# A gated two-layer transformer block in fp32: the second pass's query projection by two levels of seven products

## The chip, the cores and the metric

The kernel runs on one core of a Trainium2 chip. The metric is the device time of one execution in microseconds; the median over several runs counts, and lower is better. All arithmetic is fp32.

## The reference

The input `x` is 8 batches of 256 tokens with 1024 features. Four residual layers follow each other, each gated by a tanh: an autocorrelation attention against a context, a feed-forward layer with low-rank additions, a cross-attention, and a last feed-forward layer. The change concerns the third:

```python
q = (layernorm(x) @ wq).reshape(bs, s, 32, 128).transpose(0, 2, 1, 3)   # 32 query heads
k = (ctx @ wk).reshape(bs, s, 8, 128).transpose(0, 2, 1, 3)             # 8 key heads
v = (ctx @ wv).reshape(bs, s, 8, 128).transpose(0, 2, 1, 3)
q, k = rope(q), rope(k)
w = softmax(where(mask, q @ k.T / sqrt(128), -1e9))     # four query heads per key head
x = x + tanh(g) * ((w @ v) @ wo)
```

`wq` is 1024 x 4096 and `wo` is 4096 x 1024.

## The kernel before

**Passes and steps.** The 8 batches are done in two passes of four batches (1024 tokens), and each pass goes through all four layers. In the cross-attention a pass has two blocks of 512 tokens (two batches each) and 8 key heads. A step is one block and one key head: it makes the queries of the four query heads (`queries`, L968), the scores and softmax (`scores`, L1124), the weighted values (`values`, L1161), and then the output projection (`outputs` L989 in the first pass, `outputs_of_two` L1016 in the second). The 16 steps go block by block, and in each block head by head.

**Seven products.** The large projections use a scheme that multiplies two matrices cut into 2 x 2 quarters by seven products of quarters instead of eight. It needs sums of quarters on both sides beforehand (`left_operands` L206 for weights, `right_operands` L215 for tokens: four sums each) and sums of the products afterwards (`combine`, L223: per seven products one copy on ScalarE and seven sums on VectorE). The order of the products is `SEVEN = (1, 2, 6, 7, 4, 5, 3)`. For the queries the quarters are over 512 of 1024 features and two of four heads, and over tokens of one batch of the block's two. A product then is two accumulation groups of four matmuls of 128 x 128 by 128 x 256, into a PSUM tile of the pool `at_mm`, which has four (L855). The output projection of the second pass uses two levels of this scheme, 49 products for a pair of key heads, with weight sums (`wo2_d`) that the first pass makes on GpSimd (`finer_weights`, L912) and keeps in HBM.

**Rope.** `combine` leaves each finished quarter of the queries in PSUM. `rope` (L709) then takes three operations on VectorE that read it (L714 to L716) and one addition on GpSimd (L717), and the tile with the queries is ready for the scores.

**Sums of tokens and weights.** `query_operands` (L824) normalizes a block (VectorE), transposes it (TensorE, copies on ScalarE) and makes the token sums (VectorE). The first pass's steps over its first block make the sums of `wq` and `wo` (VectorE, L863 and L885) and store them in HBM (`wq_d`, `wo_d`); later steps load them.

**Order.** The code is written as generators. In each step the four quarter-steps `(n, l)` do scores, then a number of products of the next step's queries (`q_fill`), then values of the quarter-step before with some products of the outputs (`o_fill`) in between. A scheduler then places the instructions on each engine, so that an engine's queue differs somewhat from the order in the code. Each engine works through its queue in order, and all transfers shown here are issued from SyncE's (SP) queue, in order too; an SP transfer that waits holds up those behind it.

Of the kernel before, what the change touches and what calls it, by code (L numbers as in the profile page):

```python
# [46 lines left out]
def flamingo_kernel(ctx: ExitStack, tc: tile.TileContext, a: dict, out: bass.AP):  # L47
# [54 lines left out]
    wo2_d = [dram.tile([P, 7, 2, 2, 2, S], F32, name=f"wo2_d{i}") for i in range(N_KV // 2)]  # L102

# [249 lines left out]

    def normed(dst, xt, mv, rstd, i):
        nc.vector.tensor_scalar(
            dst, xt, mv[:, i, 0:1], rstd[:, i : i + 1], ALU.subtract, ALU.mult
        )
# [25 lines left out]
    def autocorrelation(p, xt, pools, beside, late):  # L383
# [12 lines left out]
        def normalize(b0, b1):  # L396

            n = b1 - b0
            mv, rstd = norm_stats(xt[b0 * 2 : b1 * 2])
            lin = stats.tile([P, 2 * n, 2], F32, tag="lin", name="lin", bufs=2)  # L400
            nc.vector.tensor_copy(lin[:, :, 0], rstd[:, : 2 * n])
            nc.vector.scalar_tensor_tensor(
                lin[:, :, 1], mv[:, : 2 * n, 0], -1.0, rstd[:, : 2 * n], ALU.mult, ALU.mult
            )
            for b in range(n):
                norms[b0 + b] = lin[:, b * 2, :], lin[:, b * 2 + 1, :]
# [302 lines left out]
    def rope(dst, x, cos, sin, pool):  # L709

        H = P // 2
        t = pool.tile([P, 2, S], F32, tag="rope", name="rope", bufs=1)
# [136 lines left out]

    def attention(p, xt, groups, keep, norms, xops, ahead):  # L850
        gq, go, gx = groups
        with (
# [8 lines left out]
            paired = p == NPASS - 1  # L861

            def load_wq(step):  # L863
# [12 lines left out]
                else:  # L876
                    ops = {}
                    where = {1: a["wq"][g, 0, 0], 2: a["wq"][g, 0, 1], 4: a["wq"][g, 1, 1]}
                    where |= dict(zip((5, 7, 6, 3), wq_d[g]))
                    for r in SEVEN:  # L880
                        ops[r] = big_tile(gq, [2, KH, DH], f"wq_{r}")
                        nc.sync.dma_start(ops[r], where[r])
                wq[step] = ops

# [45 lines left out]
            def stream_wo():  # L930

                places = []
                for _, g in steps[::2]:
                    for n, r in enumerate(SEVEN):
# [33 lines left out]
            def queries(step, qT):  # L968
# [3 lines left out]
                for r in SEVEN:  # L972
# [11 lines left out]
                    if done:  # L984
                        qT[done[1]] = half("qT", 7)
                        rope(qT[done[1]], done[0], tab_q[:, 0, :], tab_q[:, 1, :], w1)
                    yield

# [204 lines left out]
            fine = nothing  # L1193
            new_xl = lambda: big_tile(gx, [D], "xl")
            if paired:
                wo_stream = stream_wo()
            load_wq(steps[0])
            load_kv(steps[0])
            qT = {}
            for _ in queries(steps[0], qT):  # L1200
                pass
            norms[1] = norm_stats(xt[NBT:])
            load_wq(steps[1])
# [3 lines left out]
            if paired:  # L1207
                q_fill = {0: (2, 2, 1, 1), 1: (2, 2, 2, 1), end: (0, 0, 0, 0)}
                o_fill = {k: (0, 5, 10, 10) if k % 2 == 0 else (3, 5, 8, 8) for k in range(end)}
                o_fill[end] = (6, 6, 6, 6)  # L1210
# [6 lines left out]
            def start_outputs():  # L1217
                if paired:
                    got = outputs_of_two(last[0][0][0], [oT for _, oT in last])
# [7 lines left out]
            for k, step in enumerate(steps):  # L1227
                follow = k + 1 < len(steps)
                following = {}
                if follow:  # L1230
                    load_kv(steps[k + 1])
                    q_gen = queries(steps[k + 1], following)
                    if k == 0:
                        fill_from(q_gen, 1)
                else:
                    q_gen = nothing
                for i, (n, l) in enumerate(((0, 0), (0, 1), (1, 0), (1, 1))):
                    got = scores(step, l, n, qT)
                    nq = q_fill.get(k, (3, 3, 1, 0))[i]
                    no = o_fill[k][i]  # L1240
                    fill_from(q_gen, nq)
                    mid = min(no, middle)
                    if i > 0:
                        fill_from(o_gen, no - mid)
                    if before is not None:
                        values(*before, lambda: fill_from(o_gen, mid))
# [7 lines left out]
                    if i == 2 and k + 2 < len(steps):  # L1254
# [7 lines left out]
                    if i == 0 and p == 0 and step[0] > 0 and step[1] % 2:  # L1262
                        fine = finer_weights(step)
# [313 lines left out]
```

## Time and profile before

| what | value |
|---|---|
| median of 3 runs | 3332.11 us (3331.08 to 3334.94) |
| the profiled execution | 3335.22 us, its span 3333.4 us |
| TensorE busy | 3265.3 us, 98% |
| VectorE busy | 2217.8 us, 67% |
| GpSimd busy | 1412.0 us, 42% |
| ScalarE busy | 1051.6 us, 32% |
| moved by DMA | 505.55 MB, mean 152 GB/s |
| cross-attention, first pass | its first queries start at 534.7 us |
| cross-attention, second pass | its first queries start at 2205.9 us, its last output products at about 3227 us |

A matmul in fp32 shows up as two instructions in the trace. TensorE's matmuls overlap, so that the mean time of one (379 ns for 128 x 256) is longer than the distance between two of them. A stretch's row names, in this order, its length, the busy time and number of instructions of TensorE, of its weight loads, of VectorE, ScalarE and GpSimd, the granted TensorE clock, the share of the DMA engines and GB/s. A row of groups has the line, engine, operation, tiles and shapes, the count, the busy time and the mean of one in ns, and then the engine's idle time before these instructions with what ended it.

### The profile page before, as it was taken

The page shows a single profiled execution, that of the slowest core. Times are in us where ns is not written, and L with a number is a line of the kernel's source. Part 1 is how long each engine was busy: PE and PEld are TensorE (multiplying, and loading weights), DVE is VectorE, ACT ScalarE, POOL GpSimd, SP SyncE. Part 2 cuts the span into 40 slices and gives each one's busy share as a digit, 9 for nine tenths or more (in the row PEclk, how much of TensorE's full clock was granted, in tenths as well). Part 3 has the DMA queues.
Part 4 walks back from the last instruction along what each step waited for, and adds up shares of the span by engine and source line. Part 5 has one row for each costly group of instructions (what it writes and reads, how often), then busy time and mean ns, then how long its engine had stood idle before and what let it go on. Part 6 is the DMA issues. An engine that isn't in the chain of part 4 may idle for free. (4 is left out here: it accounts for less than half of the span.)

```text
span 3333.4 us, 39399 instructions
## 1 busy us (share of the span) xinstructions
PE 3265.3 (98%) x13456; PEld 2406.4 (72%) x13456; DVE 2217.8 (67%) x4305; ACT 1051.6 (32%) x2555; POOL 1412.0 (42%) x1181
## 2 busy tenths in 40 slices
PE   8999999999999999999999999999999999999999
PEld 6677557777677767775456677568888888888874
DVE  7787757867776655564647686456676766666773
ACT  1333112433333433334113231115333334334420
POOL 4554211333322475476344542112454454454662
PEclk9999999999999999999999999999999999999999
DMA  7533705333333354554443434043554455555551
GB/s 278 175 117 120 273 32 193 136 130 137 135 125 128 133 212 152 175 206 161 144 162 117 144 115 165 7 163 99 164 184 160 161 169 173 167 168 171 177 187 51
DMA packets 216933, 505.55 MB, mean 152 GB/s; under 512 B 25204, under 2 KB 103028, under 8 KB 216734
## 3 DMA queue, kind: packets, MB, share of 16 engines
q1 hardware_dynamic: 215582, 498.84, 44.2%
q0 software_dynamic: 1152, 4.19, 0.3%
q8 instruction: 108, 1.77, 0.2%
q14 instruction: 91, 0.75, 0.1%
HBM read 394.96 MB, written 108.00 MB: 151 GB/s over the span
## 5 line engine op out<-in xcount | busy, mean ns | idle before, releaser
L717 POOL TENSOR_TENSOR qT<-qT,rope 128x512 f32<-128x512 f32 x128 | 170.0, 1328 | 786.9 <-DVE qT L716 747.1
L976 PE MATMUL ps_q<-xn,wq 128*128 128x256 f32 x1920 | 428.9, 379 | 0.0
L976 PEld LDWEIGHTS ps_q<-xn,wq 128*128 128x128 f32 x1920 | 364.8, 190 | 50.5 <-PE po L677 0.5
L1146 ACT ACTIVATE s<-s,nmx 128x256 f32<-128x256 f32 x512 | 255.9, 500 | 244.7 <-DVE nmx L1143 244.5
L1141 DVE COPY_PREDICATED s<-keep,ps_s 128x512 f32<-128x512 uint8 x256 | 184.9, 726 | 156.4 <-PE ps_s L1132 155.5
L976 PE MATMUL ps_q<-xn_t,wq 128*128 128x256 f32 x1280 | 285.6, 379 | 0.0
L370 DVE SCALAR_TENSOR_TENSOR x<-po,tg,x 128x512 f32<-128x512 f32 x248 | 177.3, 743 | 136.8 <-PE po L677 42.2
L976 PEld LDWEIGHTS ps_q<-xn_t,wq 128*128 128x128 f32 x1280 | 243.2, 190 | 33.1
L1173 ACT COPY wT<-pt 128x512 f32<-128x512 f32 x256 | 138.8, 585 | 362.4 <-PE pt L1167 362.4
L1132 PE MATMUL ps_s<-kT,qT 128*128 128x256 f32 x1024 | 247.9, 379 | 0.0
L1178 PE MATMUL av<-wT,v 128*128 128x256 f32 x1024 | 245.7, 382 | 1.7 <-ACT wT L1173 1.6
L1155 ACT ACTIVATE s<-s,tot 128x256 f32<-128x256 f32 x512 | 230.2, 497 | 39.9 <-DVE tot L1153 39.8
L1178 PEld LDWEIGHTS av<-wT,v 128*128 128x128 f32 x1024 | 191.4, 190 | 54.6 <-issue 22.2
L1068 PE MATMUL po<-wo,oI 128*128 128x256 f32 x896 | 215.6, 381 | 2.0 <-issue 1.2
L1132 PEld LDWEIGHTS ps_s<-kT,qT 128*128 128x128 f32 x1024 | 191.8, 190 | 25.1 <-issue 0.5
L1005 PE MATMUL po<-wo,oT 128*128 128x512 f32 x448 | 201.3, 592 | 0.0
L1068 PEld LDWEIGHTS po<-wo,oI 128*128 128x128 f32 x896 | 169.2, 191 | 25.7 <-issue 2.0
L1186 ACT COPY oT<-av 128x512 f32<-128x512 f32 x128 | 74.9, 585 | 355.1 <-PE av L1178 353.5
L253 POOL TENSOR_TENSOR x<-x,part 128x512 f32<-128x512 f32 x48 | 75.3, 1570 | 249.1 <-ACT part L252 249.1
L1143 DVE TENSOR_REDUCE nmx<-s 128x2 f32<-128x512 f32 x256 | 173.2, 682 | 6.9
L1068 PE MATMUL po<-wo,oT 128*128 128x256 f32 x672 | 172.8, 384 | 1.9 <-DVE co L1083 0.3
L1005 PEld LDWEIGHTS po<-wo,oT 128*128 128x128 f32 x448 | 82.7, 190 | 82.5 <-issue 74.1
(290 smaller groups left out, 6401.7 us busy)
## 6 DMA issues: line engine op xcount, KB each, us to landing
wo<-wo_d SPq DMA_DIRECT2D x144, 512.0 KB, 4.6
wq<-in_wq_dram SPq DMA_DIRECT2D x104, 512.0 KB, 3.5
wq<-wq_d SPq DMA_DIRECT2D x96, 512.0 KB, 3.3
wo<-in_wo_dram SPq DMA_DIRECT2D x56, 512.0 KB, 3.5
wo_d<-fine_t SPq DMA_DIRECT2D x56, 512.0 KB, 3.3
wo<-wo_d SPq DMA_DIRECT2D x96, 256.0 KB, 3.5
w<-w_d SPq DMA_DIRECT2D x36, 512.0 KB, 5.7
wo<-in_wo_dram SPq DMA_DIRECT2D x72, 256.0 KB, 3.4
```

The source lines that it names most:

```text
L370: nc.vector.scalar_tensor_tensor(xs, ps, g, xs, ALU.mult, ALU.add)
L717: nc.gpsimd.tensor_add(dst, dst, t)
L976: nc.tensor.matmul(ps[:, l, :], wops[r][:, l, c, :], xo[r][:, c, :], start=(c == 0), stop=(c == KH - 1),)
L1005: nc.tensor.matmul(po, ops[r][:, h, t * P : (t + 1) * P], wops[r][:, h, :], start=(h == 0), stop=(h == 1),)
L1068: nc.tensor.matmul(po, left[r2][:, h, :], w[:, h, :], start=(h == 0), stop=(h == 1))
L1132: nc.tensor.matmul(ps[:, t, :], qT[i, n][:, l, t * P : (t + 1) * P], kT[:, n * S : (n + 1) * S], start=True, stop=True,)
L1141: nc.vector.copy_predicated(s, keep[b], ps)
L1143: nc.vector.tensor_reduce(nmx, s, AX.X, ALU.max, negate=True)
L1146: nc.scalar.activation(s[:, t, :], s[:, t, :], AF.Exp, bias=nmx[:, t : t + 1], accum_out=tot[:, t : t + 1],)
L1155: nc.scalar.activation(s[:, t, :], s[:, t, :], AF.Copy, scale=tot[:, t : t + 1])
L1173: nc.scalar.copy(wT[i], pt)
L1178: nc.tensor.matmul(av[:, i, :], kv[step][1][:, n * 2 + c, :], wT[i][:, c, :], start=(c == 0), stop=(c == 1),)
```

## The change

In the second pass the queries are made by two levels of seven products, for a pair of key heads and both blocks of tokens at once: the outer level cuts features, heads and tokens once (as before, but over both blocks and both key heads), the inner level cuts each of the seven products again. A pair takes 49 products of two groups of two matmuls; four pairs make 196 products, where 16 steps made 112 products of two groups of four. The steps of the second pass change their order to go through a pair of heads before the next.

- `finer_queries`: the first pass's steps over its first block load the weight operands of both heads of a pair, make four differences or sums for each of the seven (GpSimd), and store them in HBM (`wq2_d`). The stores of one round are issued at the start of the next.
- `second_block`: before the second pass's steps, the second block is normalized (ScalarE), transposed and summed (VectorE) while the first 14 products run, and both blocks' operands are combined: two differences each on VectorE and two on GpSimd, seven times, all stored in HBM (`x2_d`).
- `queries_of_all`: all 196 products, each with its weight operand and (after the first 14) its token operand loaded into one tile of a pool of seven; `combine` for the inner level, then sums of the outer level in PSUM or in kept tiles, and `rope`.
- `q_fill` and `o_fill` of the second pass are set anew, and one product of the queries is placed between the transposes and the values.

```diff
+            if paired:
+                order = (0, 0), (0, 1), (1, 1), (1, 0)
+                steps = [(blk, g + i) for g in range(0, N_KV, 2) for blk, i in order]
...
+            def finer_queries(g):
...
+                coming, before = load(0), None
+                yield
+                for n in range(7):
+                    q00, q01, q10, q11 = this = coming
+                    if before:
+                        store(n - 1, before)
+                    nc.gpsimd.tensor_add(q11, q10, q11)
+                    nc.gpsimd.tensor_sub(q10, q00, q10)
+                    if n < 6:
+                        coming = load(n + 1)
+                    yield
+                    nc.gpsimd.tensor_sub(q00, q11, q00)
+                    nc.gpsimd.tensor_sub(q01, q01, q00)
+                    before = this
+                    yield
+                store(6, before)
...
+            def second_block(kept, qT):
...
+                sums = Steps(nc.vector)
+                s = [big_tile(go, [KH, S], f"xn_t{i}") for i in (1, 2, 4)]
+                ops = right_operands(sums, q, *s)
+                late = {}
+                for n, r in enumerate(SEVEN):
+                    if n < 4:
+                        sums.run((0, 2, 1, 3)[n])
...
+                    nc.vector.tensor_sub(t1, b[1], b[0])
+                    nc.vector.tensor_sub(t2, b[3], t1)
+                    flat = [t.rearrange("p b s -> p (b s)") for t in (t1, t2)]
+                    nc.sync.dma_start(x2_d[n][3][:, 0], flat[1])
+                    nc.sync.dma_start(x2_d[n][2][:, 0], flat[0])
+                    late[n] = b, t2
+                    kept[0] += 1
+                    yield
+                while len(qT.get(steps[0], {})) < 4:
+                    yield
+                for n, r in enumerate(SEVEN):
+                    b, t2 = late[n]
+                    nc.gpsimd.tensor_sub(b[1], b[3], b[1])
+                    nc.sync.dma_start(x2_d[n][1], ops[r].rearrange("p (k c) s -> p k (c s)", k=2))
+                    nc.gpsimd.tensor_sub(t2, t2, b[2])
+                    nc.sync.dma_start(x2_d[n][4][:, 0], t2.rearrange("p b s -> p (b s)"))
...
+                    yield
+                kept[0] = 7 * 7 * N_KV // 2
...
+            def queries_of_all(kept, qT, places):
...
+                            while len(ops) < min(m + 7, kept[0]):
+                                load()
...
+                            for l in range(2):
+                                for c in range(KQ):
+                                    nc.tensor.matmul(
+                                        ps[:, l, :],
+                                        w[:, l, c, :],
+                                        x[:, c, :],
+                                        start=(c == 0),
+                                        stop=(c == KQ - 1),
+                                    )
+                            at = {2: (0, 0), 5: (1, 1), 3: (0, 1), 4: (1, 0)}.get(r)
+                            dest = lambda ps: u1[at] if r1 == 1 else ps
+                            done = combine(r, ps, tiles, lambda tag: half(tag, 1), dest)
+                            if done and r1 != 1:
+                                u, w = u1[at], w1_[at] if r1 in (7, 4, 5) else None
+                                if r1 == 7:
+                                    nc.vector.tensor_add(w, ps, u)
+                                if r1 in (6, 5):
+                                    nc.vector.tensor_add(u, ps, u)
+                                if r1 == 4:
+                                    nc.vector.tensor_sub(ps, w, ps)
+                                if r1 in (2, 5, 3):
+                                    nc.vector.tensor_add(ps, ps, w if r1 == 5 else u)
+                                if r1 in (2, 4, 5, 3):
+                                    step = {2: (0, g), 4: (0, g + 1), 5: (1, g + 1), 3: (1, g)}[r1]
+                                    q = next(places["q"])
+                                    rope(q, ps, tab_q[:, 0, :], tab_q[:, 1, :], w1)
+                                    qT.setdefault(step, {})[at] = q
+                            yield
...
+                q_gen = queries_of_all(kept, qT, places)
+                sums = second_block(kept, qT)
+                next(sums)
+                for _ in range(14):
+                    next(q_gen)
+                    next(sums)
+                for _ in sums:
+                    pass
...
-                q_fill = {0: (2, 2, 1, 1), 1: (2, 2, 2, 1), end: (0, 0, 0, 0)}
-                o_fill = {k: (0, 5, 10, 10) if k % 2 == 0 else (3, 5, 8, 8) for k in range(end)}
-                o_fill[end] = (6, 6, 6, 6)
+                q_fill = {k: (3 + (k % 4 == 1), 3, 3, 3) for k in range(end)}
+                q_fill[0] = 6, 6, 6, 6
+                q_fill |= {end - 2: (2, 2, 2, 1), end - 1: (1, 1, 1, 1), end: (0, 0, 0, 0)}
+                o_fill = {k: (4, 7, 7, 7) if k % 2 == 0 else (6, 6, 6, 6) for k in range(end + 1)}
...
+                    if i == 3 and p == 0 and k % 2 == 0 and k < N_KV:
+                        fine_q = finer_queries(k)
+                    fill_from(fine_q, 1)
```

In the first pass `queries` stays, and its `rope` gets two buffers instead of one.

## The prediction

> **What bounds the kernel now.** I read the engine totals first, then stretches of the second pass's attention (it runs from 2206 to about 3230 us), then who waits for whom in it, then the rows that price the edited operations. From the page:
>
> ```profile
> span 3333.4 us, 39399 instructions
> PE 3265.3 (98%) x13456; PEld 2406.4 (72%) x13456; DVE 2217.8 (67%) x4305; ACT 1051.6 (32%) x2555; POOL 1412.0 (42%) x1181
> ```
>
> TensorE (PE) is busy all the time: only less work there, or a new wait, moves the end. By stretch, the first being the first pass's steps over its first block, the others groups of steps of the second pass:
>
> ```profile
> 527.00:1000.00 473.00, 472.07 (x1950) 347.30 (x1949) 350.56 (x533) 169.50 (x447) 145.16 (x106) 1.00 0.40 142
> ...
> 2310.00:2543.00 233.00, 232.59 (x1128) 203.60 (x1127) 154.35 (x289) 89.03 (x240) 106.10 (x100) 1.00 0.50 161
> 2543.00:2778.00 235.00, 234.16 (x1152) 204.36 (x1151) 164.02 (x303) 91.24 (x242) 115.01 (x110) 1.00 0.53 171
> sum 968.00, PE 966.00 PEld 845.46 DVE 658.91 ACT 386.27 POOL 440.21; mean PE 161.00 PEld 140.91 DVE 109.82 ACT 64.38 POOL 73.37
> ```
>
> The columns are PE, weight loads, VectorE, ScalarE, GpSimd, clock, DMA share, GB/s. The reader is to see full TensorE, VectorE at 68% (658.9 of 968), and full clock. TensorE's waits in the whole stage are 3 us:
>
> ```profile
> PE po L1068 <- issue: 1.2, 1, 1.2
> PE po L1068 <- DVE co L1076: 0.8, 1, 0.8
> PE pt L365 <- DVE xn L355: 0.4, 1, 0.4
> ```
>
> The prices, from the groups by form and, last, TensorE's timeline:
>
> ```profile
> L244 DVE TENSOR_TENSOR ps_q<-ps_q,u 128x512 f32<-128x512 f32 x64 | 44.7, 698 | 109.0 <-PE ps_q L976 109.0
> L714 DVE TENSOR_TENSOR rope<-ps_q,tab_q 64x512 f32<-64x512 f32 x128 | 88.7, 693 | 6.8 <-POOL qT L717 0.7
> L717 POOL TENSOR_TENSOR qT<-qT,rope 128x512 f32<-128x512 f32 x128 | 170.0, 1328 | 786.9 <-DVE qT L716 747.1 <-DVE rstd L351 22.8 <-PE ps_s L1132 10.0
> L1095 DVE TENSOR_TENSOR co<-co 128x512 f32<-128x512 f32 x16 | 12.4, 774 | 0.0
> L211 DVE TENSOR_TENSOR wq_s<-wq_s,wq 128x1024 f32<-128x1024 f32 x8 | 16.9, 2114 | 0.0
> L209 DVE TENSOR_TENSOR wq_s<-wq,wq 128x1024 f32<-128x1024 f32 x8 | 9.7, 1219 | 1.4 <-DMA wq<-in_wq_dram 1.4
> ```
>
> ```profile
> 2219.68 7.07 PE L976 MATMUL ps_q<-xn_t,wq 128*128 128x256 f32 x32
> 2226.59 7.07 PE L976 MATMUL ps_q<-xn,wq 128*128 128x256 f32 x32
> ```
>
> Thirty-two matmul instructions start 6.91 us before the next 32: 0.216 us each. The 379 ns in a row are of overlapping ones.
>
> **The change, part by part.**
>
> TensorE. A step's queries were 7 products of 8 matmuls; 16 steps make 896. Now two key heads and both blocks take 49 products of 4, four times: 784. The 112 that go are 224 instructions of the trace: 224 x 0.216 = **-48.4 us**. The second block's 32 transposes (3.5 us), eight copies and four sums move from step 6 to the start, past the first scores; they are in the counts below. Groups of two matmuls instead of four should cost nothing: the outputs' groups are of two, and 8 of theirs take from 2645.88 to 2647.61, again 0.216.
>
> VectorE. For two heads and both blocks it combined 4 x 7 operations and turned 16 tiles of queries by 3: 76. Now the inner level takes 49, the outer 28, the ropes 48: 125. The 49 more, four times, are 196 x 0.69 = 135 us; 14 token differences at 0.77 add 11; four normalizations (0.96 each) go to ScalarE. Together +142: 801 us in about 920, or 87%. None of that is free unless TensorE never waits for it.
>
> Here a rule speaks against the change. Before, a step's queries kept PE 24.2 us and VectorE 19 x 0.69 = 13.1, and the trace shows TensorE waiting for VectorE for almost nothing; on that evidence the 48 us stay whole. The Trainium skill, "Trainium Kernel Development and Optimization", section Best Practices, warns that faster matmuls do not empty PSUM any faster. Now 49 products are 84.7 us of PE against 125 x 0.69 = 86.3 of VectorE: by the rule the queries run at VectorE's pace wherever no other matmuls stretch them. By the trace alone the next two items are 0 and the whole sum comes to -29; by the rule they cost 35. I go by the rule, since the row is of a ratio of 0.54 and this is 1.02. I counted the changed kernel's order of instructions by quarter-step (from one pair of score tiles to the next), each at its row's duration.
>
> - Steps 4 to 7: PE 238.4, VectorE 210.5 in all, but unevenly. The third and fourth quarter of step 4 and the first of step 5 hold PE 11.2 + 13.0 + 19.9 = 44.1 against VectorE 15.8 + 17.0 + 22.3 = 55.1. A product waits until the one four before it is emptied (`at_mm` has four tiles, and a tile is held through the outer sum and the three rope operations). Followed through these quarters, PE waits 3.2, 0.4 and 2.1 us, about 6; the last quarter of step 6 (11.2 against 15.8) adds 1. Steps 8 to 11 are the same. Steps 2 and 3 give 1, steps 12 to 15 about 4: **+19**.
> - The start: 14 products before the first scores, then steps 0 and 1. PE 124.4, VectorE 135.7, and VectorE comes 4.4 us late (it ends its old work at 2210.3, the queries start at 2205.9). Products 15, 16 and 17 wait for ropes, 3.5 + 3.7 + 1.8; later PE 24.2 meets VectorE 35.3, and with some 4 us of slack 7 go: **+16**.
> - There GpSimd's 14 differences run beside VectorE's 18 sums in SBUF. The row of L211 shows 2.11 us where its like takes 1.22: it runs while GpSimd adds (763.5 to 765.8, and GpSimd's two adds beside it take 2.51 and 2.25 instead of 1.27). If all 18 paid, 16 us (0.9 each); if none met, 0. Of the four sums that `left_operands` makes, L211 alone pays so, and the operations that read PSUM do not; about a third: **+5**.
> - The second level's rope has one buffer: the next waits for GpSimd's add, 1.33 us after. Two ropes often lie 1 to 1.5 us apart. Bounds: 0, and 64 x 0.7 (the only such wait in the trace) = 45 if all lay on the path. Only the dense quarters count: **+4**.
>
> The first pass. GpSimd gets 112 differences of 1.3 us, 146 us on top of 145 in 473; SyncE's queue gets 224 transfers of 256 KB, 58.7 MB: 142 GB/s becomes 266, the share 0.40 becomes 0.75. Behind a difference that waits for its load stand, on GpSimd, the rope's adds (for the scores), the outputs' operands and the residual adds; behind a store that waits for GpSimd stand, on SP, loads of `wq`, `wo`, keys and values. In a step from 732 to 798 us the `wo` loads land 28 us ahead of use and GpSimd has a hole of 24 us where 14 differences need 18; the closest rope add ends 6.5 us before its scores. Bounds: 0, and 5 us in each of 8 steps, 40. It is nearest to the holes: **+7**.
>
> Transfers of the second pass: a step's queries load 12.25 products x 2 x 0.262 = 6.4 MB instead of 7 x 0.524 = 3.7; with 6.4 of `wo` and 0.5 of keys and values it moves 13.3 MB instead of 10.6, 171 GB/s becomes 232, share 0.72. Twelve products in a row in step 0 want 6.3 MB in 20.7 us, 304 GB/s, where the busiest slice of the page moves 278: 2 us short, and the seven tiles ahead help: **+3** (0 to 15). Those loads read sums from HBM that must have landed; in SP's queue eleven stores that wait for GpSimd stand just ahead of them, and behind them keys, values and `wo`. The new order of the steps moves as many keys and values as before: 0.
>
> ScalarE (12 copies, 8 normalizations more) stays under half busy: 0; uncovered it would be 13 us.
>
> Sum: -48.4 + 19 + 16 + 5 + 4 + 7 + 3 = +5.6. The profiled execution took 3335.2 us (span 3333.4), 3.1 above the median of 3332.1. Against the median: **3338 us**.
>
> **The rivals.**
>
> *The tiles give slack enough.* VectorE's 87% stays under PE, TensorE waited 3 us in a stage where VectorE had single quarters at 80 to 100%, and GpSimd's holes take the differences. Then the stalls halve, 19 + 16 to 18, and the small terms come to 6: -48.4 + 24 = -24, 3308 us. Against it: three dense quarters in a row never occur before.
>
> *The first pass's queues block (slower).* A round of four differences reuses tiles whose stores must land (3.3 us) before the next loads (3.4) can start, then 5.2 us of work. Where a round holds GpSimd past the rope's margin of 6.5 us, TensorE waits for scores. At 2 us in half the quarter-steps of eight steps (16) that is 32 instead of 7: 3363 us. For it: one in-order queue, DMA at 0.75. Against: the 28 us margins of the weights.
>
> *It does not save what it says.* If short groups pay the 0.241 us that the busy time of L1068 gives (215.6 / 896) instead of 0.216, 1568 instructions lose 38 us: 3376. The timeline speaks against it.
>
> **How the numbers follow.** Forecast 0.51, its own range 3325 to 3352; slack 0.31; queues 0.15; no saving 0.03. A measurement here tells 0.2%, 6.7 us, from no change. The forecast gives 0.04 faster, 0.19 same, 0.28 slower; slack 0.30 faster, 0.01 same; the others 0.18 slower: 0.34, 0.20, 0.46. Leaving out 0.1 at either end, below in the slack case and above in the last two, and with the terms' bounds: 3304 to 3366.
>
> **What would show it.** Right: `ps_q` matmuls of the second pass at 1568 instructions, PE's busy time in the stage down by about 48, waits of PE for VectorE (`ps_q`, rope, `co`) of 30 to 45 us, most in the first 120 us and in every fourth and fifth step; VectorE near 85%. Wrong: such waits under 15 us (slack), PE idle between 527 and 1000 us above 10 (queues), waits for DMA on `q_ops` (my +3), or a pitch of the new matmuls above 0.216.

## The result, and the profile after

The changed kernel takes 3367.01 us, the median of its runs (3364.31 to 3371.43). Its ratio to the kernel before is 1.0101, with a 95% interval of 1.0087 to 1.0116: slower by 34 us. The forecast was 3338, its range ended at 3366.

First the page's totals, as the span and the engines' busy times.

```profile
span 3365.1 us, 40364 instructions
PE 3237.1 (96%) x13232; PEld 2371.0 (70%) x13232; DVE 2354.6 (70%) x4516; ACT 1064.4 (32%) x2574; POOL 1576.2 (47%) x1307
```

TensorE has the 224 instructions less that were counted (13456 became 13232), VectorE 137 us more and GpSimd 164. Less work for TensorE and a longer span: TensorE now waits. Where, two stretches tell; they are the first pass's steps over its first block and the second pass's whole attention stage, in the columns of before.

```profile
527.00:1000.00 473.00, 433.24 (x1729) 317.74 (x1728) 319.87 (x477) 147.73 (x392) 274.63 (x195) 0.96 0.70 242
2258.60:3258.70 1000.10, 977.59 (x4723) 849.76 (x4722) 825.95 (x1517) 404.80 (x1065) 493.84 (x478) 0.99 0.70 225
```

The same stage of the kernel before, from the first queries to the last output products, which the prediction did not show:

```profile
2205.87:3227.20 1021.33, 1017.02 (x4946) 888.74 (x4945) 698.73 (x1309) 393.88 (x1050) 486.16 (x464) 1.00 0.52 168
```

The second pass does what it was made for, in part: from the first matmul of its queries (2205.87 before, 2258.99 after) its stage takes 999.7 us instead of 1021.3, 21.6 less. The loss lies in the first stretch, where TensorE was idle 0.9 us of 473 and now is for 39.8. From the first matmul of its queries to the first of the next layer the first pass's attention took 1071.6 us (535.10 to 1606.72) and takes 1124.6 (536.65 to 1661.21), 52.9 longer. What lies before, between and behind changes by 2 us or less: 52.9 - 21.6 = 31.3, of the 31.7 by which the spans differ.

TensorE's waits in the first stretch (us in total, times, longest):

```profile
PE po L1216 <- DVE qT L729: 19.5, 5, 7.1
PE ps_q L1043 <- DVE qT L729: 15.8, 3, 7.5
PE av L1389 <- ACT wT L1384: 4.5, 2, 3.9
```

TensorE waits for the rope, VectorE's, and not for GpSimd's add behind it. The groups of VectorE in that stretch say what made the rope late:

```profile
L219 DVE TENSOR_TENSOR wq_s<-wq_s,wq 128x1024 f32<-128x1024 f32 x7 | 14.7, 2094 | 0.0
...
L217 DVE TENSOR_TENSOR wq_s<-wq,wq 128x1024 f32<-128x1024 f32 x7 | 9.7, 1380 | 41.5 <-DMA wq<-in_wq_dram 41.5
```

L217 is L209 of before, the first of the four sums of a step's raw query weights (`left_operands`). In the kernel before VectorE never waited for these loads in this stretch (its longest wait there for any load was 1.7 us, for `wo`); now it waits 41.5 us. The chain, in the timeline of the changed kernel (start, duration, engine, line; in brackets the idle time before it and what ended it; SP's rows are transfers that it issues, and the length is the time until the last of them has left the queue):

```profile
702.66 1.27 POOL L940 TENSOR_TENSOR fine_q<-fine_q 128x512 f32<-128x512 f32 x1 [7.83 <-DMA wq_d<-fine_q]
...
708.81 0.43 SPq L1024 DMA_DIRECT2D kT<-kT_d  x1
709.34 9.10 SPq L929 DMA_DIRECT2D wq_d<-fine_q  x5
718.53 0.38 SPq L891 DMA_DIRECT2D wq<-in_wq_dram  x1
...
716.82 1.27 POOL L945 TENSOR_TENSOR fine_q<-fine_q 128x512 f32<-128x512 f32 x1
...
708.08 0.69 DVE L250 TENSOR_TENSOR ps_q<-w,ps_q 128x512 f32<-128x512 f32 x1 [2.69 <-PE ps_q L1043]
722.89 1.23 DVE L217 TENSOR_TENSOR wq_s<-wq,wq 128x1024 f32<-128x1024 f32 x1 [14.12 <-DMA wq<-in_wq_dram]
724.15 0.69 DVE L727 TENSOR_TENSOR rope<-ps_q,tab_q 64x512 f32<-64x512 f32 x1
...
726.30 5.16 PE L1043 MATMUL ps_q<-xn,wq_s 128*128 128x256 f32 x16 [7.04 <-DVE qT L729]
```

Read it from below. TensorE waits 7.04 us for a PSUM tile that the rope empties. The rope stands on VectorE behind the sum of L217, which waits 14.12 us for a raw weight. That load (L891) was issued at 718.53, because the queue it shares was held for 9.10 us by five stores of finer sums (L929), which wait for GpSimd's differences: the last of the five for that of L945, which starts at 716.82 and ends at 718.09. GpSimd itself had waited 7.83 us for transfers of the same kind. SP's own waits show the new kind; in the kernel before SP waited in this stretch for TensorE and VectorE alone:

```profile
SPq L929 <- POOL fine_q L945: 84.3, 20, 8.2
SPq L891 <- PE ps_q L1043: 35.4, 14, 5.1
...
SPq L929 <- POOL fine_q L941: 17.0, 3, 7.5
SPq L929 <- POOL fine_q L946: 15.7, 13, 2.8
```

The waits cost more than their length. In the kernel before the granted clock of this stretch was 1.00 throughout. Now it is 0.50 for 6.8 us around each of the six idle gaps of 3.9 to 7.5 us, and matmuls of 256 columns start 0.427 us apart there instead of 0.216; around the gaps of 1.2 and 0.4 us it stays at 1.00. For the gap of 7.04 us above:

```profile
722.40:729.20 6.80, 2.90 (x7) 2.36 (x8) 6.11 (x9) 0.00 (x0) 1.27 (x1) 0.50 0.88 291
```

The first six steps take 54.4 us longer than before (417.5 instead of 363.1). Of these TensorE's idle time is 39.0 (39.8 instead of 0.8); the other 15 are the same instructions at the lower clock.

### The profile page after: what moved, and what is told of

It is laid out like the page before. It is cut to its first block, busy times and chain, and to the rows that moved or that the text cites. A ratio compares the mean times of both kernels' runs of the same rounds, so it can differ in the third digit from the quotient of the medians.

```text
span 3365.1 us, 40364 instructions
## 1 busy us (share of the span) xinstructions
PE 3237.1 (96%) x13232; PEld 2371.0 (70%) x13232; DVE 2354.6 (70%) x4516; ACT 1064.4 (32%) x2574; POOL 1576.2 (47%) x1307
## 5 line engine op out<-in xcount | busy, mean ns | idle before, releaser
L1173 PE MATMUL ps_q<-q_ops 128*128 128x256 f32 x1456 | 335.3, 380 | 2.5 <-issue 2.1
L1173 PEld LDWEIGHTS ps_q<-q_ops 128*128 128x128 f32 x1456 | 272.9, 190 | 39.9 <-issue 3.8
L730 POOL TENSOR_TENSOR qT<-qT,rope 128x512 f32<-128x512 f32 x99 | 129.8, 1311 | 350.9 <-DVE qT L729 321.4
L1043 PE MATMUL ps_q<-xn,wq 128*128 128x256 f32 x896 | 200.1, 379 | 0.0
L1343 PE MATMUL ps_s<-kT,qT 128*128 128x256 f32 x792 | 194.7, 382 | 1.1 <-POOL qT L730 1.0
L1043 PEld LDWEIGHTS ps_q<-xn,wq 128*128 128x128 f32 x896 | 170.2, 190 | 23.6 <-PE po L690 0.2
L1343 PEld LDWEIGHTS ps_s<-kT,qT 128*128 128x128 f32 x792 | 149.7, 191 | 21.9 <-POOL qT L730 1.4
L1378 PEld LDWEIGHTS pt<-ident,s 128*128 128x128 f32 x1024 | 122.9, 142 | 32.5 <-issue 18.0
```

The lines of the kernel that those rows point to most:

```text
L1043: nc.tensor.matmul(ps[:, l, :], wops[r][:, l, c, :], xo[r][:, c, :], start=(c == 0), stop=(c == KH - 1),)
L1173: nc.tensor.matmul(ps[:, l, :], w[:, l, c, :], x[:, c, :], start=(c == 0), stop=(c == KQ - 1),)
L1343: nc.tensor.matmul(ps[:, t, :], qT[i, n][:, l, t * P : (t + 1) * P], kT[:, n * S : (n + 1) * S], start=True, stop=True,)
L1378: nc.tensor.transpose(pt[:, c, t * P : (t + 1) * P], got[i][:, t, c * P : (c + 1) * P], ident,)
```

## The experiments

The theory, T: the new stores wait for GpSimd in SP's in-order queue and hold the raw weights of the next step, and through VectorE TensorE. Against it: R1, GpSimd's 146 us of differences delay its adds; R2, the transfers as such (share 0.70) are too much; R3, VectorE and GpSimd slow each other in SBUF.

The kernel before took 3325 to 3333 us in the sessions below, so each kernel is given by its ratio to it, and in us as that ratio times 3332.1. "Block 0" is the time of the first six steps of the first pass, from the starts of the score reductions in VectorE's timeline. "Weights" is VectorE's wait for the raw weights between 527 and 1000 us.

| kernel | ratio (95%) | us | block 0 | weights |
|---|---|---|---|---|
| before | 1 | 3332 | 363.1 | none |
| the change | 1.0101 (1.0087 to 1.0116) | 3366 | 417.5 | 41.5 |
| first pass's part alone | 1.0190 (1.0149 to 1.0231) | 3395 | 415.6 | 36.2 |
| transfers, no differences | 0.9976 (0.9959 to 0.9992) | 3324 | 371.7 | 7.4 |
| decoupled | 1.0185 (1.0149 to 1.0221) | 3394 | 411.8 | 7.5 |
| own results | 1.0008 (0.9994 to 1.0022) | 3335 | 392.2 | 8.1 |
| stores from GpSimd | 1.0212 (1.0172 to 1.0252) | 3403 | 459.4 | 53.2 |
| raw weights from ScalarE | 1.0159 (1.0135 to 1.0183) | 3385 | 428.8 | 14.1 |
| fills on GpSimd | 1.0097 (1.0073 to 1.0122) | 3364 | 422.7 | 43.9 |
| half rounds | 1.0008 (0.9993 to 1.0022) | 3335 | 387.1 | 7.7 |
| half rounds, fills on GpSimd | 1.0003 (0.9988 to 1.0018) | 3333 | 392.8 | 16.2 |
| half rounds, spread | 1.0093 (1.0077 to 1.0109) | 3363 | 378.3 | 11.0 |
| half rounds, paced | 1.0046 (1.0033 to 1.0059) | 3347 | 394.3 | 23.5 |

The last two columns come from one trace each and are less sure than the ratios. Up to the second pass's queries, "fills on GpSimd" has the change's order of instructions on every engine but for four of its fills, and so has "half rounds, fills on GpSimd" that of the half rounds; yet block 0 differs by 5.2 and 5.7 us, and the weights by 2.4 and 8.5. Smaller differences in these columns say nothing.

**The first pass's part alone.** The kernel before with `finer_queries`, the calls of it and `wq2_d`:

```
+                    if i == 3 and p == 0 and k % 2 == 0 and k < N_KV:
+                        fine_q = finer_queries(k)
                     fill_from(fine, 1)
+                    fill_from(fine_q, 1)
```

> The kernel before, with the first pass's part of the change alone (GpSimd makes and stores the finer sums of the queries' weights; the second pass doesn't use them). Theory T (SP's in-order queue is held by the new stores, which wait for GpSimd, so the next step's weights come late to VectorE and through it to TensorE): the first pass loses all of its 53 us and nothing else changes, 3385 us (3375 to 3392), 50 to 56 us of it between 535 and 1010 us. All rivals (R1: GpSimd's 146 us of work in front of rope and residual adds; R2: the transfers' share of 0.70; R3: VectorE and GpSimd slowing each other in SBUF) give the same 3385. The +7 of the prediction would be 3339. With the 3367 of the whole change it gives the second pass's part as a difference: about -18 to -21.

Block 0 loses 52.5 us (415.6 - 363.1; 54.4 in the change), and VectorE waits 36.2 us for raw weights. So the loss needs nothing of the second pass. The time, 3395 with an interval of 3382 to 3409, lies above the expected range (3375 to 3392), which the interval reaches into.

**Transfers, no differences.**

```
-                    nc.gpsimd.tensor_add(q11, q10, q11)
-                    nc.gpsimd.tensor_sub(q10, q00, q10)
...
-                    nc.gpsimd.tensor_sub(q00, q11, q00)
-                    nc.gpsimd.tensor_sub(q01, q01, q00)
```

> The whole change without GpSimd's 112 differences in the first pass: all 112 loads of two parts and 112 stores stay, the stored tiles are the loaded ones (the second pass's queries are then computed from the wrong operands, at the same cost). T: a store now waits only for a load that landed a quarter-step before, the weights come in time, 3311 to 3322 us, TensorE's waits between 535 and 1010 under 10 us. R2 (transfers as such): the loss stays, 3355 to 3367. R1 and R3 (GpSimd's work): the loss goes too, 3311 to 3318; the next kernel tells them from T.

It is faster than the kernel before, but it leaves out the differences that the second pass needs. The first stretch:

```profile
527.00:1000.00 473.00, 464.77 (x1916) 342.27 (x1915) 342.12 (x524) 167.88 (x444) 144.68 (x105) 1.00 0.75 263
```

The share of the transfers is higher than in the change (0.75 against 0.70), GpSimd is back at 145 us, and TensorE idles 8.2 us instead of 39.8. R2 falls as the main cause: the transfers alone cost 8.6 us of block 0. At 3324 it is 2 us above T's range (3311 to 3322).

**Decoupled.** As many differences, on a tile of their own, and the stores are of the loaded tiles; the first pass's rope has one buffer, where the change gave it two:

```
-                    nc.gpsimd.tensor_add(q11, q10, q11)
-                    nc.gpsimd.tensor_sub(q10, q00, q10)
+                    nc.gpsimd.tensor_add(own, own, own)
+                    nc.gpsimd.tensor_sub(own, own, own)
```

> The whole change with all the loads, stores and as many differences of the same size on GpSimd in the first pass, but the differences work on a tile of their own: no store waits for GpSimd and GpSimd waits for no load (the operands stored are the loaded ones; the first pass's rope tile has one buffer, as before the change). T: 3311 to 3328 us, since only the dependence is gone. R1 (GpSimd's time) and R3 (port): 3350 to 3367, since GpSimd's 146 us are all there, beside the same VectorE work. R2: 3355 to 3367.

By its time T had lost, but the waits of VectorE show another cause than any of the theories:

```profile
DVE rope L727 <- POOL qT L730: 73.4, 8, 21.8
```

The differences waited for nothing, so the scheduler drew them forward: in GpSimd's timeline 22 of them stand between two adds of the rope (from 619.6 to 647.2 us), and VectorE waits up to 21.8 us for its one rope tile. The first scores of the pass come 32 us late (600.2 against 568.0). It shows what GpSimd's differences cost in the wrong order when the rope has one tile, those 32 us and 48.7 more in block 0; it does not test T.

**Own results.** The differences read the loaded tiles, so that they stay where they were, and write a tile of their own (the rope again has one buffer):

```
+                    nc.gpsimd.tensor_add(own, q10, q11)
+                    nc.gpsimd.tensor_sub(own, q00, own)
...
+                    nc.gpsimd.tensor_sub(own, q11, own)
+                    nc.gpsimd.tensor_sub(own, q01, own)
```

> As the decoupled kernel, but with GpSimd's queue in the order of the change: there the scheduler had drawn the differences, which waited for nothing, 28 in a row ahead of the ropes' adds. Here the differences read the loaded tiles and write a tile of their own, so a difference still waits for its load, and the stores (of the loaded tiles) wait for no difference; SP's order of transfers is that of the change nearly one for one. (The operands stored are the loaded ones; the rope tile has one buffer.) T: SP is now held by GpSimd only where a load takes a tile that a difference still reads; the raw weights come earlier, VectorE's wait for them (41.5 us in the change) falls under 20, 3320 to 3340 us. R1 (the differences ahead of rope and residual adds) and R3 (VectorE and GpSimd in SBUF): the same work in the same order, 3355 to 3370.

3335 us, inside T's range. GpSimd's work and most of its order are those of the change, and so is SP's; but no store waits for a difference. VectorE's wait for raw weights goes from 41.5 to 8.1 us, block 0 from 417.5 to 392.2. If the parts add up, then of the loss of 54.4 us in block 0, 25 are the stores' waits for GpSimd, 9 the transfers, and the 20 between them come with GpSimd's differences, each by 6 us more or less (what two traces of the same code differ by). T is right on the largest part. The rest with GpSimd's differences can be R1 or R3, which no run separates; the single rope buffer of this kernel (10.1 us of waits on VectorE) is in it too. The lower clock is in every part: in block 0 of this kernel TensorE idles 21.5 us of 392.2, and the remaining 8 or 9 us of its loss are again the same instructions at that clock.

**Stores from GpSimd.**

```
-                        nc.sync.dma_start(
+                        nc.gpsimd.dma_start(
                             wq2_d[g // 2][:, n, i], q.rearrange("p l d -> p (l d)")
```

(and directly behind a round's differences instead of in the next round)

> The whole change, and the 56 stores of a pair's finer sums in the first pass are issued by GpSimd itself right behind its differences, instead of by SP a half quarter-step later. All work and all bytes stay. T: SP no longer waits for GpSimd, only its loads still wait for a store to land (20 us in the trace of the change), so most of the 53 us goes: 3318 to 3335 us. R1, R2, R3: nothing of their cause changes, 3355 to 3370. If issuing from GpSimd is itself slow there (1 us or more each), GpSimd's queue takes the place of SP's and the time stays above 3340.

A miss, the slowest of all. The loads of a round need tiles whose stores have landed, and those loads are still in SP's queue:

```profile
SPq L921 <- DMA wq_d<-fine_q: 117.9, 28, 9.7
```

The wait in SP's queue is of another kind and as long (117.0 us for GpSimd in the three rows of the change), and the raw weights behind it are later than ever (53.2 us). It is no clean test of T, since two sums of VectorE stand through GpSimd's work for 8.94 and 9.79 us here (last section). From 530 to 1000 us GpSimd also spends 51.1 us on issuing (92 of its 112 stores, 0.556 each).

**Raw weights from ScalarE.**

```
-                        nc.sync.dma_start(q[i][k], a["wq"][g, i, k])
+                        nc.scalar.dma_start(q[i][k], a["wq"][g, i, k])
```

> The whole change, and the raw weights of the queries in the first pass's block 0 (32 loads) are issued from ScalarE's queue instead of SP's. All work, all bytes, GpSimd's queue and its waits stay. T: these loads no longer stand behind stores that wait for GpSimd; VectorE's wait at the first sum falls from 41.5 us to under 12, TensorE's 36 us of waits for the rope behind it go, 3318 to 3335 us (what is left: the sums' tiles, stores of wq_s that still stand in SP's queue, ScalarE held by loads that wait for TensorE's last read of a tile). R1, R2, R3: nothing of their cause changes, 3355 to 3370.

VectorE's wait for them falls to 14.1 us (T said under 12), with 9.5 us more before the same sum that the profile puts down to a load of the finer sums. The time is longer than the change's:

```profile
PE av L1389 <- ACT wT L1384: 31.9, 6, 9.4
```

A raw weight waits for TensorE to be done with its tile. In ScalarE's queue that wait stands ahead of the softmax and the copies of `wT` (two of these stand 19.8 us for such loads), and TensorE waits 31.9 us for the copies. The stop moved to an engine with more behind it.

**Fills on GpSimd.** In the second pass only:

```
-                    nc.vector.memset(s, MASKED)
+                    (nc.gpsimd if paired else nc.vector).memset(s, MASKED)
```

> The whole change, and in the second pass GpSimd instead of VectorE fills the score tiles with the mask's value (128 fills, 0.485 us each on VectorE, 62 us in all; GpSimd took 0.53 for the like in the decoupled kernel). If the second pass's 27 us of lost gain are VectorE's (its dense quarters): VectorE 826 -> 764 us in the attention stage, 8 to 16 us faster than the change, 3351 to 3359. If they are transfers or the start alone: within 4 us of 3367. If GpSimd's queue matters there (the fill stands behind residual adds of 1.3 us, and the scores wait for it): slower than 3367, to 3385.

```profile
L1351 POOL MEMSET s<- 128x512 f32 x124 | 62.7, 526 | 89.4 <-PE pt L1378 49.6 <-ACT s L1357 32.2 <-DVE nmx L1354 4.3
```

Fills of 60 us leave VectorE between 2300 and 3200 us (its busy time falls from 742.3 to 697.2), and the eight steps from 4 to 12 of the second pass take 485.0 us instead of 487.8. So VectorE's sum does not set the pace of the second pass: it is worth 3 us in these steps, where TensorE idles 5.2 us in the change. The whole time (3364 against 3366) shows no difference.

**Half rounds.** The same four tiles of 512 KB a tile hold four half rounds (one row `l` of both heads) instead of two rounds, and a store follows its differences two calls later:

```
+                for t in range(14):
+                    if t < 13:
+                        tiles.append(load(t + 1))
...
                     nc.gpsimd.tensor_sub(q01, q01, q00)
+                    if t > 1:
+                        store(t - 2)
+                    yield
```

> The whole change with the same finer sums made in half rounds: a round of 2 MB becomes two of 1 MB (one row l of the heads at a time), so that the same four tiles hold four rounds in flight instead of two, and a store is issued two half quarter-steps after its differences instead of one. 224 differences of 128x256 (0.73 us each, 163 us of GpSimd in all, 17 more than the change), as many bytes, 112 loads and 56 stores on SP. T (SP's queue held by stores that wait for GpSimd): the stores find their differences done, SP's waits for GpSimd fall from 117 us to under 40 and VectorE's wait for raw weights from 41.5 to under 15; 3322 to 3338 us (3324 is what the transfers alone left). R1 (GpSimd's time before ropes and residual adds): more of it than before, 3360 to 3375. R3: the same, 3360 or more.

3335 us: 31 gained on the change, with all of its work done and 27 us more of it on GpSimd (1603.5 instead of 1576.2; 17 were expected). The rounds are of 1 MB and 512 KB, half of what the expectation says. The waits of SP and of VectorE:

```profile
SPq L923 <- POOL fine_q L937: 102.3, 34, 8.1
```

```profile
DVE wq_s L217 <- DMA wq<-in_wq_dram: 7.7, 3, 4.1
```

One expectation failed in a useful way: SP still waits 102 us for GpSimd, not under 40, and yet VectorE waits 7.7 us instead of 41.5 (3.4 more before the same sum are put down to a load of the finer sums). So the length of the queue's wait does not decide; that few of the loads behind it were needed soon is the likely reason, but the kernel also issues half as many transfers (112 loads and 56 stores, where the change has 224 and 112), and no run parts the two.

**Half rounds, fills on GpSimd.** Both edits together.

> The kernel with half rounds, and GpSimd fills the score tiles in the second pass (62 us less for VectorE there). That alone gave nothing measurable on top of the change (1.0097 against 1.0101 of the kernel before), so the theory that the second pass's steady part isn't bound by VectorE's sum says: within 4 us of the kernel with half rounds. If the first pass's late start had hidden its gain: 8 to 16 us faster than that kernel.

Within 2 us of the half rounds, as expected. Steps 4 to 12 are again 2.8 us shorter, and block 0, which the edit does not touch, is 5.7 longer.

**Half rounds, spread.** Two pairs of heads in block 0, one beside the first pass's Fourier layer and one beside the second pass's LoRA layer:

```
-                    if i == 3 and p == 0 and k % 2 == 0 and k < N_KV:
-                        fine_q = finer_queries(k)
+                    if i == 3 and p == 0 and k in (0, 4):
+                        fine_q = finer_queries(k // 2)
...
+            fine_q = finer_later(w2, [2]) if p == 0 else iter(())
```

> The half rounds, with only two of the four pairs of heads made in the first pass's block 0 (a half round per quarter-step instead of two), the third pair beside the first pass's last layer and the fourth beside the second pass's first layer, where GpSimd is busy for a fifth to two fifths and the transfers' share is 0.3 to 0.5. All the work of the change is done. T with the reading that what is left in the kernel with half rounds (some 20 us in block 0) comes from the density of transfers and stores there: block 0 loses 8 to 14 us, the two layers 0 to 10, the second pass gains its 21: 3315 to 3330 us, likeliest 3321, faster than both kernels. If the new transfers on SP hold the two layers' own loads as they held the raw weights: 3335 or more.

A miss twice over. The scheduler packed both pairs into the first steps, as the two stretches show (GpSimd's column and the share, 0.89 and 0.43):

```profile
560.00:700.00 140.00, 133.00 (x580) 104.28 (x579) 103.48 (x160) 55.38 (x150) 116.40 (x125) 0.99 0.89 302
700.00:840.00 140.00, 134.65 (x530) 96.20 (x530) 96.33 (x147) 47.76 (x126) 52.71 (x40) 0.98 0.43 148
```

Block 0 loses 15 us instead of 24, for half the work. And the stages between the two attention stages take 27 us longer than before (626.2 instead of 599.2), since there VectorE waits for GpSimd's residual adds, which now have the differences ahead of them (1580 to 2290 us; 23.4 us in the kernel before):

```profile
DVE x L389 <- POOL x L269: 40.4, 6, 13.3
DVE x L389 <- POOL x L261: 34.8, 4, 18.8
```

There it is as R1 said: GpSimd's differences delay its own adds.

**Half rounds, paced.** A tile of a half round is first touched by a copy on GpSimd that reads the quarter-step's score sums, and its loads wait for that:

```
+                    nc.gpsimd.tensor_copy(x[:, :, 0, 0:1], latest[0].unsqueeze(2))
                     for i in range(2):
                         nc.sync.dma_start(
```

> The half rounds, paced: a tile of finer sums is first touched by a small copy on GpSimd that reads the score sums of the quarter-step, and its loads wait for that copy, so the scheduler can no longer draw the rounds ahead (in the kernel with half rounds, and in the one with half the pairs elsewhere, it had packed them into the first two or three steps, where the transfers' share was 0.88 to 0.92 and 15 to 17 us were lost). T with that reading: the share stays near 0.75 in all eight steps, block 0 loses 8 to 15 us instead of 20, 3317 to 3330 us, likeliest 3325. If the loss comes from GpSimd's operations themselves wherever they lie: 3331 to 3340. If the new small waits hold SP or GpSimd: 3340 or more.

The share is 0.61 to 0.69 throughout, so the pacing works, but block 0 does not lose less: 31.2 us in six steps, against 24.0 and 29.7 in the two kernels with half rounds and no pacing, and every step but the first pays 4.5 to 7.3. The whole is 12 us slower than the half rounds. SP's waits for GpSimd grow to 186, and the raw weights are late again (23.5 us):

```profile
SPq L925 <- POOL fine_q L939: 135.7, 37, 6.4
SPq L917 <- POOL fine_q L915: 50.6, 17, 4.5
```

It is the third of the three outcomes expected, and it fits T: the small copies add waits to the queue in which the raw weights stand. No version that does all the work beat the kernel before.

## Why the prediction was right or wrong

The direction held, the size did not, and the two stages were wrong in opposite directions: the second pass stalled less than forecast, the first far more.

| term | predicted | measured | from |
|---|---|---|---|
| TensorE's instructions | -48.4 | -48.4 | 13456 - 13232 = 224, and their pitch |
| start of the second pass | 16 + 5 + 3 | 15.4 | below |
| the rest of the second pass | 19 + 4 | 11.4 | below |
| first pass | 7 (0 to 40) | 52.9 | stage marks |
| sum | +5.6 | +31.3 | the spans differ by 31.7 |

*TensorE* was right. The second pass has its 1568 instructions of `ps_q`, in three groups:

```profile
L1173 PE MATMUL ps_q<-q_ops 128*128 128x256 f32 x1456 | 335.3, 380 | 2.5 <-issue 2.1 <-DMA q_ops<-x_d 0.3
...
L1173 PE MATMUL ps_q<-xn,q_ops 128*128 128x256 f32 x64 | 16.2, 402 | 0.0
L1173 PE MATMUL ps_q<-xn_t,q_ops 128*128 128x256 f32 x48 | 13.2, 424 | 3.1 <-issue 3.1
```

In the timeline 16 of them start 3.45 us before what follows (2369.24 to 2372.69): 0.216 each, so groups of two pay nothing extra, and the third rival is out.

*The first pass*, +7 where 52.9 was measured, is the step that failed. The prediction looked for the margins of a queue and took the wrong ones: the `wo` loads, 28 us ahead of use, GpSimd's hole of 24 us and the rope add's 6.5. The load that counts is the raw `wq`, and the timeline of the kernel before has its margin, for the last of a step's four and the sum that reads it:

```profile
750.64 0.33 SPq L871 DMA_DIRECT2D wq<-in_wq_dram  x1
...
754.70 1.22 DVE L209 TENSOR_TENSOR wq_s<-wq,wq 128x1024 f32<-128x1024 f32 x1
```

This load took 3.4 us to land, so it is there at 754.1 and read at 754.7: 0.6 us to spare. In six of the seven steps of this stretch the last load is issued 4.1 us before its sum (684.65 and 688.71 the step before). What holds up such a load by more than its margin arrives at its reader, with all that stands behind the reader: here the rope, and behind the rope TensorE's PSUM tiles. The runs put some 25 of the 54 us of block 0 on stores that wait for GpSimd ahead of it (own results) and 9 on the transfers. A sign of the margin stood in the row of L209 that the prediction took its price from: 1.4 us of waiting for this load, the only wait in that row. And a stall was priced at its length; 15 of these 54 us came on top, at a granted clock of 0.50. The upper bound of 40 us was made without both, so it was no bound.

*The rival "the first pass's queues block"* named the stage, and it came out at 3363, near what was measured, but not by its mechanism. It let GpSimd delay the scores; in the changed kernel TensorE has no wait for the rope's add in that stretch. That the number is near is luck: it was off by 21 us in the first pass (32 against 52.9), and the second pass made up for that, where the stalls are 27 us, not the forecast's 47 which it kept. For the second pass the rival that the tiles give slack enough came nearest: it left 24 us for all stalls, the first pass's included, and its sign, waits of TensorE for VectorE under 15 us, came true.

*The second pass.* From the first queries to step 4, TensorE's counted work (0.216 us for each instruction of 256 columns, 0.108 for each of 128: 243.6 us after, 231.6 before) took 261.0 and 233.6: 17.4 us of stalls where there were 2.0, so 15.4 new ones for the three start terms of 24. Steps 4 to 12 have 10.8 instead of 5.0 us beyond the counted work, and the last four with what follows 5.6 more: 11.4 for the terms of 23. The rule of the Trainium skill ("Trainium Kernel Development and Optimization", section Best Practices), that faster matmuls do not empty PSUM faster, asked for 35 in two of these terms, where the trace of before by itself asked for 0. (The skill says it of tiling on TensorE; here it was carried over to fewer matmuls.) The sum of all the second pass's stalls, 27, lies between the 12 that are left without these terms and the 47 with them, but in the steady part the pace of VectorE is not its reason: fills of 60 us less on VectorE brought 3 us in eight steps, and the waits of TensorE that the profile puts down to VectorE come to 5.0 us in the whole stage, against the 30 to 45 that were to show the forecast right. The largest group is 5.2 us of "issue", of which 4.9 lie in the start and are read below. The term for the second level's single rope tile was not too small:

```profile
L727 DVE TENSOR_TENSOR rope<-ps_q,tab_q 64x512 f32<-64x512 f32 x62 | 43.0, 693 | 5.2 <-POOL qT L730 2.5
```

VectorE waits 2.5 us for GpSimd's add there (2300 to 3200 us), against +4. Of the 15.4 us of the start, 9.3 are idle time of TensorE (9.6 instead of 0.3), and the others are slower instructions: between 2285.7 and 2302.8 the granted clock was 0.50 for 10.2 us in all, around and behind these two waits:

```profile
2285.68 0.69 DVE L729 TENSOR_TENSOR qT<-ps_q,tab_q 128x512 f32<-128x512 f32 x1
2286.48 3.75 PE L1173 MATMUL ps_q<-xn_t,q_ops 128*128 128x256 f32 x8 [3.10 <-issue]
...
2296.74 0.69 DVE L729 TENSOR_TENSOR qT<-ps_q,tab_q 128x512 f32<-128x512 f32 x1
2297.54 1.10 PE L1173 MATMUL ps_q<-q_ops 128*128 128x256 f32 x4 [1.78 <-issue]
```

They stand before the 13th and the 16th product and end 0.1 us after the last operation of a rope that reads PSUM, as the waits that are put down to the rope do in the first pass (725.55 + 0.69, and 726.30 above). So they are likely the waits for ropes that the prediction had before products 15 to 17 (9.0 us in its sum), though the profile names no cause. The transfers' share was 0.82 between 2258.6 and 2352.7 us; what they cost there stays open, since no run took them away.

*Contention*, which was priced only at the start of the second pass, belongs to the first as well. The four sums of a step's `wq` take 43.7 us in seven steps instead of 40.1, and L225, the first of the four sums of `wo`, has a mean of 1.83 instead of 1.22 us.

## What to carry to other kernels

When transfers are added to an in-order queue, list for each transfer already in it the time from its landing to its first reader, and take the smallest; the largest says nothing. A store that waits for an engine makes that engine a part of every later load of the queue, and moving it, or the loads, to another queue only moved the stop in both tries here; to give the ring more and smaller rounds, with half as many transfers, brought back 31 of 34 us here, and which of the two did it is open. Price a stall of the busiest engine by more than its length until a trace shows the clock that is granted around it: here 39 us of waits cost 54. Work that waits for nothing is not free of cost where a scheduler may draw it ahead of work that others wait for.

## What the runs showed of the hardware that was not expected

A sum of two SBUF tiles on VectorE can stand through a whole run of GpSimd's operations, and GpSimd does not pay. In the kernel with stores from GpSimd one 128x1024 sum took 8.94 us where its like takes 1.22:

```profile
741.22 8.94 DVE L217 TENSOR_TENSOR wq_s<-wq,wq 128x1024 f32<-128x1024 f32 x1 [13.46 <-DMA wq<-in_wq_dram]
...
740.51 1.27 POOL L939 TENSOR_TENSOR fine_q<-fine_q 128x512 f32<-128x512 f32 x1
741.73 1.27 POOL L217 TENSOR_TENSOR oS<-oT 128x512 f32<-128x512 f32 x1
742.95 1.26 POOL L943 TENSOR_TENSOR fine_q<-fine_q 128x512 f32<-128x512 f32 x1
744.17 1.25 POOL L218 TENSOR_TENSOR oT<-oT 128x512 f32<-128x512 f32 x1
745.39 1.25 POOL L219 TENSOR_TENSOR oS<-oS,oT 128x512 f32<-128x512 f32 x1
746.61 1.25 POOL L944 TENSOR_TENSOR fine_q<-fine_q 128x512 f32<-128x512 f32 x1
747.83 1.25 POOL L220 TENSOR_TENSOR oS<-oT,oS 128x512 f32<-128x512 f32 x1
```

Seven GpSimd operations follow one another without a gap, each at its own 1.25 to 1.27 us, and the sum ends 1.1 us after the last of them. A second sum in this kernel, at 904.25, took 9.79 us beside seven more. The Trainium skill ("SBUF — State Buffer", section SBUF: two separate sides) says that the two engines share a pair of ports by a lock that is held for one instruction, and that the loser blocks. By that alone the sum would have waited for at most one operation, some 2.5 us; the trace shows that it need not get its turn between two of them. In the kernel before the two had met once a step, and the sum took 2.29 us at most.
